# A selective-scan and attention block on one core: the front of the next image pair beside the phases behind a pair's scan

## The chip, the cores and the metric

The kernel runs on one core of a Trainium2 chip. The metric is the device time in microseconds (us) of one execution. The host only lays the inputs out, in one launch.

## The reference

Eight images of 96 channels and 64 x 64 points go through two layers. Shortened to what is computed:

```python
# layer 0: group norm, then a four-direction selective scan
xh = layernorm(gn(x) as tokens); xi, z = split(xh @ in_proj_w.T + in_proj_b)   # 192 + 192
xi = silu(depthwise_conv3x3(xi) + conv_b)
for k in range(4):                       # row order, column order, and both reversed
    dts, Bs, Cs = split(x_proj_w[k] @ xs[k])
    delta = softplus(dt_proj_w[k] @ dts + dt_proj_b[k])
    h_t = exp(delta_t * A) * h_(t-1) + delta_t * u_t * B_t        # 16 states a channel
    y_k = sum_n(h_t * C_t) + D * u
y = layernorm(sum of the four, back in row order) * silu(z)
x = x + (y @ out_proj_w.T + out_proj_b)
# layer 1 on the 4096 tokens of an image
t = x as tokens
t = t + attention(layernorm(t))          # linear: (q k^T / 4) v, no softmax, 6 heads
t = t + ffn(layernorm(t))                # 96 -> 384 -> 96, operands rounded to fp8 (5, 2)
```

Since the attention has no softmax, k^T v (16 x 16 for each head) is summed over all tokens first, and q times that sum is folded with the output weights into one 97 x 96 matrix for an image.

## The kernel before

The images go in four pairs. A pair's 4096 points are cut into 8 chunks of 512 (`F`, `NCH`). For each pair the function at the end of `vss_attn_ffn` calls, one after the other, `front`, `prepare`, `scan`, `back` and `tail`; each opens its own pools in SBUF and PSUM and closes them, and what passes between the stages lies in SBUF (`xi`, `t1`) or in scratch tensors in DRAM (`zs`, `us`, `dl`, `du`, `bs`, `cs`, `ys`).

- `front` loads an image (L240 statistics, L256 group norm), norms each chunk (L261 and L265 matmuls, L263 square, L267 Ln, L268 Exp, L269 and L270), projects it (L297, L299, L313 matmuls; L300 and L305 put the result into the padded images `ybuf`, L317 is the Silu of z, which goes to DRAM), and convolves: 9 taps on VectorE over whole images for two of the three tiles (`taps`, L281 and L283, then Silu, L286), and 9 diagonal matmuls a chunk for the third (L331, with Silu in the evacuation, L335). Its PSUM ring has four banks.
- `prepare` stores `xi` as `us` (L343 with `spread`), makes delta, its products and its three bf16 parts, and stores them.
- `scan` is under an order written out by hand. TensorE makes the decays (L553), ScalarE exponentiates them (L557), GpSimd makes the drive (L535), VectorE scans (L570), TensorE sums over the states (L588).
- `back` takes 16 steps, one for a chunk of an image. A step loads `z3`, `ut`, `xr` and `yk` (1.57 MB, four directions), adds directions (L686 on VectorE, L687 on GpSimd), transposes and sums them on TensorE into `py` (L691: two matmuls of 512 columns; L700: 64 small ones, four of which stand in different column groups), copies (L705, L707), norms (L713 `yc`, L716 square, L720 `yv`, L724, L725), gates (L729, L732), projects (L735 `po`) and adds the input (L738), into `t1` in SBUF. An fp32 matmul shows as two records in the profile. Each of `py`, `yc`, `yv`, `po` has two PSUM banks.
- `tail` first norms every chunk of `t1` into `tn` (L755 to L763) and sums k^T v (L780 `pk`, L785 `kv`, L789 `pm`); then forms the matrix `hm` for each image (L797 to L806); then runs the feed-forward over 16 steps, three at a time, as generators (L814 `pa`, L816, `norm`, L823 to L827, L831 to L838, store at L839).

Outside of `scan` a scheduler puts the instructions of each engine in order, from the order in the program and its own estimate of when operands are ready. All DMAs are issued by SP, in one order. Exp and Ln are in one table of ScalarE, Silu and Softplus in two others; a token (`stamp_issue_order_token`) keeps a table load in place.

Of the kernel before, what the change touches and what calls it, by code (L numbers as in the profile page):

```python
# [10 lines left out]
F32 = mybir.dt.float32  # L11
# [40 lines left out]
def vss_attn_ffn(ctx: ExitStack, tc: tile.TileContext, a: dict):  # L52
# [119 lines left out]
    def half(T):  # L172
        return 1 if T == 2 else 0

    def decay_weights():
# [42 lines left out]
    def front(pair, xi, zs, ybuf):  # L218
        with ExitStack() as st:
            p1 = st.enter_context(tc.tile_pool(name="p1", bufs=1))  # L220
            tmp = st.enter_context(tc.tile_pool(name="p1t", bufs=2))
            ps = st.enter_context(tc.tile_pool(name="p1ps", bufs=4, space=PSUM))

            diag = p1.tile([128, 9, 128], F32, name="diag")
            for t in range(9):
                nc.vector.tensor_scalar(
                    diag[:, t, :], ident, convw[:, 0, t : t + 1], None, ALU.mult
                )
            pad = [t.rearrange("p (h w) -> p h w", w=HH + 2) for t in ybuf]
            for t in ybuf:  # L230
                nc.gpsimd.memset(t, 0.0)

            xts = []
            for b in range(2):
                xt = p1.tile([DIM, L], F32, name="xt", bufs=2)
                xts.append(xt)
                nc.sync.dma_start(xt, x[2 * pair + b])
                bst = tmp.tile([DIM, NCH, 6], F32, name="bst")
                for c in range(NCH):
                    nc.vector.bn_stats(bst[:, c, :], xt[:, bass.ts(c, F)])  # L240
                mv = tmp.tile([DIM, 2], F32, name="mv")
                nc.vector.bn_aggr(mv, bst.rearrange("p c s -> p (c s)"))
                gps = ps.tile([128, F], F32, name="gps", tag="ps")
                nc.tensor.matmul(gps[:DIM, 0:1], gmat, mv[:, 0:1], start=True, stop=True)
                gm = tmp.tile([DIM, 1], F32, name="gm")
                nc.vector.tensor_copy(gm, gps[:DIM, 0:1])
                gd = tmp.tile([DIM, 1], F32, name="gd")
                nc.vector.tensor_tensor(gd, mv[:, 0:1], gm, ALU.subtract)
                gv = tmp.tile([DIM, 1], F32, name="gv")
                nc.vector.scalar_tensor_tensor(gv, gd, gd, mv[:, 1:2], ALU.mult, ALU.add)  # L250
                vps = ps.tile([128, F], F32, name="vps", tag="ps")
                nc.tensor.matmul(vps[:DIM, 0:1], gmat, gv, start=True, stop=True)
                gr = tmp.tile([DIM, 1], F32, name="gr")
                nc.scalar.activation(gr, vps[:DIM, 0:1], AF.Ln, bias=eps5[:DIM])
                nc.scalar.activation(gr, gr, AF.Exp, scale=-0.5)
                nc.vector.tensor_scalar(xt, xt, gm, gr, ALU.subtract, ALU.mult)  # L256

                for c in range(NCH):
                    cs = bass.ts(c, F)
                    cps = ps.tile([128, F], F32, name="cps", tag="ps")  # L260
                    nc.tensor.matmul(cps[:DIM], c96, xt[:, cs], start=True, stop=True)  # L261
                    sq = tmp.tile([DIM, F], F32, name="sq")
                    nc.scalar.activation(sq, cps[:DIM], AF.Square)  # L263
                    vp = ps.tile([128, F], F32, name="vp", tag="ps")
                    nc.tensor.matmul(vp[:DIM], j96, sq, start=True, stop=True)  # L265
                    rs = tmp.tile([DIM, F], F32, name="rs")
                    nc.scalar.activation(rs, vp[:DIM], AF.Ln, bias=eps5[:DIM])  # L267
                    nc.scalar.activation(rs, rs, AF.Exp, scale=-0.5)  # L268
                    nc.vector.tensor_tensor(xt[:, cs], cps[:DIM], rs, ALU.mult)  # L269
                    nc.vector.tensor_scalar(xt[:, cs], xt[:, cs], nw, nb, ALU.mult, ALU.add)  # L270


            def taps(T):

                for t in range(9):
                    dy, dx = divmod(t, 3)
                    w = convw[:, half(T), t : t + 1]
                    v = pad[T][:, dy : dy + HH, dx : dx + HH]
                    o = xi[T].rearrange("p (h w) -> p h w", w=HH)
                    if t == 0:  # L280
                        nc.vector.tensor_scalar(o, v, w, None, ALU.mult)  # L281
                    else:
                        nc.vector.scalar_tensor_tensor(o, v, w, o, ALU.mult, ALU.add)  # L283
                for c in range(NCH):
                    xc = xi[T][:, bass.ts(c, F)]
                    nc.scalar.activation(  # L286
                        xc, xc, AF.Silu, bias=convb[:, half(T) : half(T) + 1]
                    )

            for b in range(2):  # L290
                xt = xts[b]
                lo = slice(64 * b, 64 * b + 64)
                for c in range(NCH):
                    cs = bass.ts(c, F)
                    r0 = c * ROWS
                    pm = ps.tile([128, F], F32, name="pm", tag="ps")
                    nc.tensor.matmul(pm, winT[:, 0:128], xt[:, cs], start=True, stop=True)  # L297
                    pl = ps.tile([128, F], F32, name="pl", tag="ps")
                    nc.tensor.matmul(pl[lo], winT[:, 128:DI], xt[:, cs], start=True, stop=True)  # L299
                    nc.scalar.activation(  # L300
                        pad[b][:, r0 + 1 : r0 + 1 + ROWS, 1 : HH + 1],
                        pm.rearrange("p (h w) -> p h w", w=HH),
                        AF.Identity, bias=inb[:, 0:1],
                    )
                    nc.scalar.activation(  # L305
                        pad[2][lo, r0 + 1 : r0 + 1 + ROWS, 1 : HH + 1],
                        pl[lo].rearrange("p (h w) -> p h w", w=HH),
                        AF.Identity, bias=inb[lo, 1:2],
                    )
                    zt = tmp.tile([DIM, 2, F], F32, name="zt")  # L310
                    for g in range(2):
                        pz = ps.tile([128, F], F32, name="pz", tag="ps")
                        nc.tensor.matmul(  # L313
                            pz[:DIM], winT[:, DI + g * DIM : DI + (g + 1) * DIM], xt[:, cs],
                            start=True, stop=True,
                        )
                        nc.scalar.activation(  # L317
                            zt[:, g], pz[:DIM], AF.Silu, bias=inz[:, g]
                        )
                    nc.sync.dma_start(zs[b, :, :, cs].rearrange("g p l -> p g l"), zt)  # L320

                if b == 0:
                    taps(0)

            taps(2)
            for c in range(NCH):
                r0 = c * ROWS
                pc = ps.tile([128, F], F32, name="pc", tag="ps")
                for t in range(9):
                    dy, dx = divmod(t, 3)  # L330
                    nc.tensor.matmul(  # L331
                        pc, diag[:, t, :], pad[1][:, r0 + dy : r0 + dy + ROWS, dx : dx + HH],
                        start=(t == 0), stop=(t == 8),
                    )
                nc.scalar.activation(xi[1][:, bass.ts(c, F)], pc, AF.Silu, bias=convb[:, 0:1])  # L335
# [10 lines left out]
    def prepare(pair, xi, us, dl, du, bs, cs_):  # L346
        with ExitStack() as st:
# [8 lines left out]
            for o in range(2):  # L356
                for c in range(NCH):
# [12 lines left out]
                    for k in (o, o + 2):  # L370
# [12 lines left out]
                        for T in range(3):  # L383
# [5 lines left out]
                            act = nc.scalar.activation(  # L389
                                d, pq, AF.Softplus, bias=dtb[:, k, half(T) : half(T) + 1]  # L390
                            )
# [22 lines left out]
            tc.stamp_issue_order_token(act.ins, f"tables{pair}")  # L414


    def scan(pair, dl, du, bs, cs_, ys):
        with ExitStack() as st:
            st.enter_context(tc.manual_schedule())

            act = nc.scalar.preload_act_table_set(LOGEXP)
            tc.stamp_issue_order_token(act.ins, f"tables{pair}")
# [121 lines left out]
            def decay(p):  # L544
# [12 lines left out]
                act = nc.scalar.activation(e, e, AF.Exp)  # L557
                if p == 0:
                    tc.stamp_issue_order_token(act.ins, f"tables{pair}")
# [64 lines left out]
            for s in range(N + 2):  # L624
                for v in range(8):
# [22 lines left out]
                    next(more, None)  # L648


    def back(pair, ys, us, zs, t1):
        with ExitStack() as st:
            tmp = st.enter_context(tc.tile_pool(name="bk", bufs=2))
            psy = st.enter_context(tc.tile_pool(name="bky", bufs=2, space=PSUM))
# [88 lines left out]
    def tail(pair, t1):  # L743
        with ExitStack() as st:
# [5 lines left out]
            def bank(name):  # L750
                return ps.tile([128, F], F32, name=name, tag="ps")
# [233 lines left out]
```

## Time and profile before

| | us |
|---|---|
| median of 3 runs | 12261.4 (12260.9 to 12297.62) |
| profiled execution | 12263.4 |
| its span | 12261.5 |
| VectorE busy | 8797.7 |
| TensorE busy | 8871.2 |
| GpSimd busy | 7971.1 |
| ScalarE busy | 6823.8 |

The page lists for each line of the kernel the engine, the operation, the tiles, how often it ran, its busy time and mean duration, and the idle time before it with what ended it. A table by stretches shows the same busy times for any part of the span. The granted clock is the share of TensorE's full clock that the chip let through; matmul durations in the trace grow as it falls, and a mean over several stretches mixes both. A record of the trace is one instruction[...].

### The profile page before, as it was taken

The numbers are of one execution on the slowest core, as the hardware profiler recorded it, in microseconds if no ns is written. First come the engines' busy times: TensorE is split into PE (matmuls) and PEld (weight loads), VectorE is DVE, ScalarE is ACT, GpSimd is POOL, SyncE is SP. The second block draws the span as 40 slices with busy tenths as digits, with TensorE's granted clock in tenths as the row PEclk, the third lists the DMA queues.
The fourth block names the chain that finished last, engine by engine and source line by source line (L and its number), as shares of the span: only waits on it lengthen the run. The fifth ranks groups of instructions, "written<-read, shape, count | busy, mean of one in ns | idle before, by whom it ended". The sixth has DMA issues, their size and how long they took to land. (4 is left out here: it accounts for less than half of the span.)

```text
span 12261.5 us, 386934 instructions
## 1 busy us (share of the span) xinstructions
PE 8871.2 (72%) x170112; PEld 5730.0 (47%) x170112; DVE 8797.7 (72%) x6393; ACT 6823.8 (56%) x12095; POOL 7971.1 (65%) x2750
## 2 busy tenths in 40 slices
PE   6856666678886666667888666666778766666777
PEld 2245555543225555554322555555432255555543
DVE  4489999952448899995244899989424499999942
ACT  3566666633456666663345666666333566666623
POOL 0489999941048999993114899999300499999931
PEclk9678888887767878888775888888877688888887
DMA  2988888872298888887129888888712988888871
GB/s 74 203 199 199 199 198 198 198 164 49 63 211 200 199 194 197 203 198 154 41 73 203 198 200 198 198 196 201 157 36 67 217 198 200 198 199 203 199 157 24
DMA packets 1627242, 2042.53 MB, mean 167 GB/s; under 512 B 958083, under 2 KB 1303252, under 8 KB 1622740
## 3 DMA queue, kind: packets, MB, share of 16 engines
q1 hardware_dynamic: 1625556, 2017.78, 72.0%
q8 instruction: 1335, 21.87, 0.9%
q14 instruction: 351, 2.88, 0.1%
HBM read 1579.00 MB, written 438.38 MB: 165 GB/s over the span
## 5 line engine op out<-in xcount | busy, mean ns | idle before, releaser
L570 DVE TENSOR_TENSOR_SCAN h<-da,dbu 128x774 f32<-128x774 f32 x4096 | 7027.3, 1760 | 665.5 <-ACT da L557 522.2
L535 POOL TENSOR_TENSOR dbu<-dut,bc 128x1536 f32<-128x1536 f32 x2048 | 7084.7, 3504 | 594.0 <-ACT dbu L532 515.2
L557 ACT ACTIVATE da<-da 128x768 f32<-128x768 f32 x4096 | 3257.9, 798 | 2166.0 <-PE da L553 2123.5
L588 PE MATMUL yp<-h,cw 128*32 128x48 f32 x131072 | 3142.9, 246 | 1130.8 <-issue 1115.7
L553 PE MATMUL da<-dm,aw 128*128 128x128 bf16 x24576 | 2508.0, 251 | 1458.0 <-DVE h L570 1076.1
L588 PEld LDWEIGHTS yp<-h,cw 128*32 128x32 f32 x131072 | 2545.6, 155 | 1699.1 <-issue 1431.7
L553 PEld LDWEIGHTS <-aw 128*128 128x128 bf16 x24576 | 1846.8, 111 | 1768.5 <-issue 1439.4
L489 ACT ACTIVATE cw<-bc,blk 128x512 f32<-128x512 f32 x2048 | 1475.1, 722 | 309.8 <-DMA bc<-cs 230.5
L408 POOL TENSOR_TENSOR dp<-rest,dp 128x512 bf16<-128x512 f32 x384 | 458.4, 1194 | 718.7 <-ACT dp L407 688.0
L406 DVE TENSOR_TENSOR rest<-delta,dp 128x512 f32<-128x512 f32 x384 | 302.5, 789 | 674.5 <-ACT dp L405 674.5
L687 POOL TENSOR_TENSOR yk<-yk 128x768 f32<-128x768 f32 x64 | 143.5, 2243 | 942.4 <-DMA yk<-ys 480.4
L365 POOL COPY u<-xi 128x512 f32<-128x512 f32 x96 | 111.0, 1170 | 982.7 <-PE pc L331 653.4
L385 PE MATMUL pq<-S,dtw 12*128 12x512 f32 x768 | 594.8, 882 | 167.0 <-ACT S L377 91.6
L838 POOL TENSOR_TENSOR ot<-t,y 96x512 f32<-96x512 f32 x64 | 73.5, 1148 | 944.1 <-DVE y L836 929.1
L596 ACT ACTIVATE yev<-yp 128x384 f32<-128x384 f32 x1024 | 503.6, 492 | 242.6 <-PE yp L588 240.9
L385 PEld LDWEIGHTS pq<-S,dtw 12*128 12x128 f32 x768 | 162.5, 251 | 596.6 <-ACT delta L389 182.8
L407 ACT ACTIVATE dp<-rest 128x512 bf16<-128x512 f32 x384 | 241.4, 630 | 323.6 <-DVE rest L406 323.6
L532 ACT COPY dbu<-h 128x12 f32<-128x12 f32 x1984 | 408.3, 206 | 0.0
L729 DVE SCALAR_TENSOR_TENSOR g<-yc,c_onw,yrs 96x512 f32<-96x512 f32 x128 | 89.8, 741 | 443.3 <-ACT yrs L725 443.3
L707 ACT ACTIVATE yt<-py 128x512 f32<-128x512 f32 x64 | 38.2, 597 | 662.9 <-PE py L700 590.1
L700 PE MATMUL py<-ident,yk 128*24 128x128 f32 x8192 | 291.1, 310 | 26.4 <-DVE yk L686 26.2
L700 PEld LDWEIGHTS py<-ident,yk 128*24 128x24 f32 x8192 | 256.8, 118 | 113.5 <-DVE yk L686 78.2
(131 smaller groups left out, 6892.3 us busy)
## 6 DMA issues: line engine op xcount, KB each, us to landing
dut<-du SPq DMA_DIRECT2D x1024, 768.0 KB
dm<-dl SPq DMA_DIRECT2D x512, 576.0 KB
dl<-dp SPq DMA_DIRECT2D x256, 384.0 KB
dm<-dl SPq DMA_DIRECT2D x512, 192.0 KB
ys<-yev SPq DMA_DIRECT2D x1024, 96.0 KB
du<-du SPq DMA_DIRECT2D x256, 256.0 KB
bc<-bs SPq DMA_DIRECT2D x512, 128.0 KB
bc<-cs SPq DMA_DIRECT2D x512, 128.0 KB
```

Of the source, the lines that this page charges most:

```text
L385: nc.tensor.matmul(pq, dtw[64:76, k, T], S[64:76], start=True, stop=True)
L406: nc.vector.tensor_tensor(rest, d, dp[:, :, 0], ALU.subtract)
L408: nc.gpsimd.tensor_tensor(dp[:, :, 2], rest, dp[:, :, 1], ALU.subtract)
L489: nc.scalar.activation(cw[i % 2][:, :, :, m, :].rearrange("p z j t -> p (z j) t"), bc[i][:, 1].rearrange("p z (j t) -> p (z j) t", j=NB), ...
L532: nc.scalar.copy(start, segs(hs[s - 1][:, :, r])[:, :, :, 1 if back else TC])
L535: nc.gpsimd.tensor_tensor(segs(t)[:, :, :, 1:], dut[g // 2][:, NI * (r % 2) : NI * (r % 2) + NI, :].unsqueeze(1) .to_broadcast([128, 2, NI ...
L553: nc.tensor.matmul(e[:, i], aw[k, r][:, i, z, :], dm[s][:, NI * r + i, :], start=True, stop=True,)
L557: act = nc.scalar.activation(e, e, AF.Exp)
L570: nc.vector.tensor_tensor_scan(hs[s][:, w, r][:, d], da[p % 3][:, o : o + W6][:, d], dbu[4 * s + r][:, w][:, d], 0.0, ALU.mult, ALU.add,)
L588: nc.tensor.matmul(y[32 * q : 32 * q + 32, 2 * NE * i : 2 * NE * i + 2 * NE] .rearrange("p (j r i) -> p i j r", j=2, r=NR), w[:, z, :, t], ...
L596: nc.scalar.activation(yev[s][:, :, o : o + 8, :].rearrange("p j i e -> p i j e"), y[:, 0 : 16 * NE].rearrange("p (i j e) -> p i j e", j=2 ...
L700: nc.tensor.matmul(o, yk[:, k, 4 * g + e, NE * j : NE * j + NE], ident, start=False, stop=(k + j == 4),)
```

## The change

The loop over pairs now runs `npair + 1` times. In round n the phases behind the scan of pair n - 1 and the front of pair n run together, in two parts, and then `prepare` and `scan` of pair n follow as before. `front` is cut into generators: `project` (load, norm, projection; 34 pieces) and `convolve` (19 pieces), and the Silu of the convolution becomes a function of its own, `gates`. `back` and `tail` are generators too, and `together` takes pieces of one and of the other in turn:

```diff
+    def together(one, other, n, m):
+        done = 0
+        for i in range(n):
+            next(one, None)
+            while done * n < (i + 1) * m:
+                next(other, None)
+                done += 1
...
+                one = other = none
+                if old:
+                    one = back(
+                        pair - 1, old["ys"], old["us"], old["zs"], old["t1"], old["tn"],
+                        pool("bk", 2), pool("bky", 1, space=PSUM), pool("bkc", 2, space=PSUM),
+                        pool("bkm", 1, space=PSUM), pool("bkp", 2, space=PSUM),
+                    )
+                if new:
+                    other = project(
+                        pair, new["zs"], ybuf, pool("p1", 1, side="right"),
+                        pool("p1t", 2, side="right"), pool("p1ps", 2 if old else 6, space=PSUM),
+                    )
+                together(one, other, 16 if old else 1, 34)
...
+                if old:
+                    one = tail(
+                        pair - 1, old["t1"], old["tn"], pool("tt", 3), pool("tps", 6, space=PSUM)
+                    )
+                if new:
+                    other = convolve(
+                        xi, ybuf, pool("p1c", 1, side="right"), pool("p1cp", 2, space=PSUM)
+                    )
+                together(one, other, 18 if old else 1, 19)
...
+                gates(xi)
+                prepare(xi, new["us"], new["dl"], new["du"], new["bs"], new["cs"])
```

PSUM is divided anew: `py` has one bank, `yc` two, the attention sums of both images one, and `yv`, `po` and all of the attention part share a ring of two; `project` has two more beside `back` and six in the first round. The attention sums follow each chunk of `back` one step later, and `t1` and `tn` pass through DRAM:

```diff
+            def heads(i, b, ta):
+                c = i // 2
+                to = tns[i % 3]
+                norm(ta, to[0:DIM], tmp, bank)
+                nc.sync.dma_start(tn[b, :, bass.ts(c, F)], to[0:DIM])
+                for n in range(2):
+                    pk = bank("pk")
...
+                    ta = tmp.tile([DIM, F], F32, name="ta")
+                    nc.vector.scalar_tensor_tensor(ta, po[:DIM], outb, xr, ALU.add, ALU.add)
+                    nc.sync.dma_start(t1[b, :, cs], ta)
+                    if late:
+                        heads(*late)
+                    late = (2 * c + b, b, ta)
+                    yield
...
             def ffn(b, c):
                 cs = bass.ts(c, F)
+                to = tns[(2 * c + b) % 4]
+                nc.sync.dma_start(to[0:DIM], tn[b, :, cs])
+                ta = tmp.tile([DIM, F], F32, name="ta")
+                nc.sync.dma_start(ta, t1[b, :, cs])
                 pa = bank("pa")
-                nc.tensor.matmul(pa[:DIM], hm[b], tn[b][:, cs], start=True, stop=True)
+                nc.tensor.matmul(pa[:DIM], hm[b], to, start=True, stop=True)
```

The taps run over half images, a chunk of the diagonal matmuls stands behind every second tap and is evacuated without Silu, and `gates` applies it afterwards. Table loads are placed by one helper for the whole program, which keeps Ln/Exp, Silu and Softplus in the order in which the program names them:

```diff
+    def table(kind, emit):
+        if kind == "ln" and loaded[0] != "ln":
+            act = nc.scalar.preload_act_table_set(LOGEXP)
+            tc.stamp_issue_order_token(act.ins, "tables")
+        loaded[0] = kind
+        act = emit()
+        if act is not None:
+            tc.stamp_issue_order_token(act.ins, "tables")
...
+        for T in (0, 2):
+            for t in range(9):
+                dy, dx = divmod(t, 3)
+                w = convw[:, half(T), t : t + 1]
+                for h in (0, HH // 2):
...
+                if t % 2:
+                    chunk()
+                yield
+
+    def gates(xi):
+        for c in range(NCH):
+            for T in range(3):
+                xc = xi[T][:, bass.ts(c, F)]
+                b_ = 0.0 if T == 1 else convb[:, half(T) : half(T) + 1]
+                table("silu", lambda: nc.scalar.activation(xc, xc, AF.Silu, bias=b_))
```

`prepare` and `scan` change only in how they name their table loads. What each piece computes is the same as before.

## The prediction

> **What bounds the kernel now.** I read the page first, then the table by stretches for the border between the first and the second pair, then one step of the second half in order of time. The page:
>
> ```profile
> PE 8871.2 (72%) x170112; PEld 5730.0 (47%) x170112; DVE 8797.7 (72%) x6393; ACT 6823.8 (56%) x12095; POOL 7971.1 (65%) x2750
> ...
> DVE  4489999952448899995244899989424499999942
> ...
> PEclk9678888887767878888775888888877688888887
> ...
> L570 DVE TENSOR_TENSOR_SCAN h<-da,dbu 128x774 f32<-128x774 f32 x4096 | 7027.3, 1760 | 665.5 <-ACT da L557 522.2
> ```
>
> Four times the digits of DVE fall from 9 to 2 or 4 and come back: four scans of about 1900 us each, bound by DVE (and POOL), with some 1110 us of other stages between two of them. The change leaves the scan alone, so only those stages count. The stretches from one scan's end to the next one's begin (columns: stretch, length, busy us of PE, PEld, DVE, ACT, POOL with instruction counts, granted clock, DMA share, GB/s):
>
> ```profile
> 2582.00:2861.00 279.00, 225.87 (x2370) 114.39 (x2370) 89.58 (x112) 49.85 (x81) 34.17 (x16) 0.90 0.76 149
> 2861.00:2947.00 86.00, 71.91 (x324) 44.76 (x324) 12.49 (x23) 43.44 (x80) 6.95 (x2) 0.94 0.00 1
> 2947.00:3125.00 178.00, 133.23 (x194) 36.98 (x194) 60.47 (x147) 64.89 (x112) 18.26 (x16) 0.52 0.06 17
> 3125.00:3150.00 25.00, 0.94 (x5) 0.82 (x5) 20.74 (x23) 0.46 (x2) 11.17 (x4) 0.50 0.56 134
> 3150.00:3222.00 72.00, 57.94 (x66) 15.54 (x66) 24.78 (x41) 28.43 (x47) 0.00 (x0) 0.50 0.00 0
> 3222.00:3289.00 67.00, 66.32 (x132) 19.92 (x131) 28.08 (x11) 46.82 (x68) 0.00 (x0) 0.92 0.30 88
> 3289.00:3352.00 63.00, 62.22 (x146) 27.22 (x145) 50.30 (x12) 16.04 (x26) 0.76 (x1) 1.00 0.18 56
> 3352.00:3690.00 338.00, 275.16 (x384) 71.60 (x383) 149.88 (x198) 189.90 (x322) 147.56 (x122) 0.66 0.96 215
> ```
>
> In order: back, attention sums, feed-forward, load of x, layer norm, in-projection, convolution, prepare. The first seven take 770 us and PE is the busiest engine in six of them; but it runs at half clock in two (0.52, 0.50), where it waits in chains through ACT and DVE. So overlap can win twice: waits are filled, and the clock may rise. Prepare runs at DMA share 0.96 and stays as it is. One step of back:
>
> ```profile
> 2702.93 3.69 PE L700 MATMUL py<-ident,yk 128*24 128x128 f32 x128
> ...
> 2706.57 3.67 PE L713 MATMUL yc<-yt,c 128*96 128x512 f32 x8
> ...
> 2710.08 1.94 PE L720 MATMUL yv<-sq,j 96*96 96x512 f32 x4
> ...
> 2711.86 1.88 PE L691 MATMUL py<-ut,dpad 96*128 96x512 f32 x4
> ...
> 2715.55 1.96 PE L735 MATMUL po<-g,c_woT 96*96 96x512 f32 x4 [1.81 <-DVE g L732]
> ...
> 2717.44 3.69 PE L700 MATMUL py<-ident,yk 128*24 128x128 f32 x128
> ```
>
> An undisturbed step is 14.51 us (2702.93 to 2717.44), nearly all PE: 20 records of 512 columns and 128 small ones. The 16 steps take 255 us, 16 each: lower clock and late yk account for the rest.
>
> [...] The trace shows 1283 ns for each of its loads[...].
>
> **The change, part by part.** PE prices at full clock: a 512-column fp32 record is 0.43 us (convolution: 144 records in 62 us), a small py record 0.027 (3.42 us of weight loads for 128), pk 0.16 and pm 0.08 by their columns.
>
> Phase one puts `project` (load, norm, in-projection of the next pair) beside `back`, and the attention sums of a chunk (`heads`) one step behind it. It replaces 279 + 86 + 25 + 72 + 67 = 529 us. PE work per step: back 20 x 0.43 + 3.4 = 12.0; heads 4 x 0.43 + 8 x 0.16 + 8 x 0.08 = 3.6; project has 192 records, 82 us, or 5.1 a step: 20.7 in all, 331 us for 16 steps. That is the floor. The waits come from smaller rings: py has one bank instead of two, yv, po, ncp, nvp, pk share two, project has two.
>
> The order holds two kinds of steps. One with two norm chunks, in us after the end of yv: cps to 0.85; py to 1.7; vp waits for its Square, which stands on ACT behind Ln and Exp (0.68, 0.63): 2.35 to 3.2; 12 small py to 3.85; po to 5.55; ncp to 6.4; nvp after its Square, 7.4 to 8.25; the second half of py waits for the DVE copy out of the only bank: 9.7 to 10.55; the second cps waits until DVE has freed its bank, behind two Ln/Exp pairs: 12.2 to 13.05; pk to 14.35; pm and vp to 16.1; py to 16.95; yc waits for ACT's copy, behind another Ln/Exp: 18.05 to 21.5; yv to 23.4. The other kind has two in-projection chunks: pm, pl, py, two pz fill the wait for g to 4.3; po and ncp to 6.85; nvp from 7.85; pk waits for Ln, Exp and the multiply, 11.3 to 12.6; pm, pl, pz, pz with their evacuations to 16.9; py to 18.6; yc waits for two Silu, a table load and the copy, 19.9 to 23.3; yv to 25.2. Mean 24.3. The clock of back is 0.90[...]; at 0.95 the 20.7 us of work grow by 1.1: I take 25.5 a step. Phase one = 19 us to the first py (2582 to 2601) + 16 x 25.5 + 10 for the last heads = 437.
>
> What hides there: 16 table loads per pair (20 us of ACT; the walk has both of a step on the chain for about 1 us[...]). DMA moves at most 3.7 MB a step (2.55 for back, 0.4 for t1 and tn, 0.8 for zs), 147 GB/s in 25 us where prepare shows 215. On SP, a step's last yk loads are queued behind the stores of t1, tn and zs, which wait for DVE and ACT; issued about 14 us into a step they are wanted 11 us later, so they land just in time. If they were 3 us late, 48 us a pair.
>
> Phase two puts the convolution beside feed-forward: 178 + 63 = 241 us before. DVE becomes the bound: 36 half taps of 2.25 us (L283, 4.48 for a whole one) less two short ones, 77, and 16 x 4.1 for feed-forward (t2, tq, three each of h16 and hq, y16), 142. In the order some 3.2 half taps stand in a step until they run out after about 11 steps. Walk of such a step: t2, hq, two half taps to 5.9; tq waits for Exp until 7.0; y16, half tap to 10.3; the three h16/hq to 12.25. So 11 x 12.3 + 5 x 10 (10.9 now at half clock) + 10 for the hm chain and the reload from DRAM = 195. PE has 9.5 us of work in such a step at full clock; at half clock it would be 19 and dense[...].
>
> Then 24 Silu of 0.7 us, taken out of the convolution's evacuation and L286, stand alone on ACT before prepare's own work: 15 us with the table load. All of us is stored at that point; before, xi0 (2.1 MB, 10 us at 215 GB/s) had gone out earlier, and prepare is DMA-bound: I add 8. Lead 23, between 15 and 35.
>
> Sum per border: 437 + 195 + 23 = 655 against 770, 115 less, three times 345. The last pair has no partner: back with heads walks to 20 us a step, I take 21: 19 + 336 + 10 = 365, the same as 279 + 86; 5 more for the DRAM reload in feed-forward. First pair: same work, the conv still follows the projections: 0, plus or minus 15. From the profiled execution's 12263.4 (span 12261.5, 2 above the median of the runs): 12263 - 345 + 5 = 11923, and with the 2 us to the median, 11920.
>
> **Rivals.** (a) Waits fill better than the walk says: 21.5 us a step, close to the PE floor, and phase two 170: 19 + 344 + 10 + 170 + 20 = 563, 207 saved three times: 11645. For it: the PE floor[...]. (b) The queues cost more[...]: 28 us a step and 215 in phase two: 477 + 215 + 23 = 715, 55 saved three times: 12100. For it: POOL's 480 us of waits for yk already now; against: DMA share well below 1. (c) Slower: in phase one the granted clock falls to half as in the feed-forward. Then a step has 41 us of PE work, 44 with the waits, phase one 733, and the time is 12800 if it lasts; the change loses from 32.7 us a step on (552 us for phase one), that is, when about half of the steps run at half clock. For it: 0.50 in both norm stages; against: back holds 0.90 with the same dense py, yc, yv. (d) The order doesn't overlap as it says: excluded as far as the order goes, since project stands between the py of back on every engine; little but a wash is left, 12260.
>
> **How the numbers follow.** Forecast 0.64, (a) 0.12, (b) 0.15, (c) 0.07, (d) 0.02. The forecast's own spread (step 24 to 27, phase two 180 to 215, lead 15 to 35) is 11800 to 12040. The range 11690 to 12130 reaches into (a) and over (b). Faster, by over 0.3% (37 us, about what a measurement of this kernel can tell): 0.91; within 0.02; slower 0.07.
>
> **What would show it.** Right: steps of py 24 to 27 us apart with yc waiting for the copy; clock 0.9 or more; feed-forward steps of 12 us with DVE at over 0.9, later 10 or less; prepare still 338 with some 20 us before its first activation. Wrong: steps under 22 or above 30, clock 0.5 in phase one, POOL waiting for yk in most steps, or a scan of another length.

## The result and the profile after

| us | before | after |
|---|---|---|
| median (4 runs each) | 12261.85 (12260.9 to 12297.62) | 11829.53 (11820.4 to 11864.4) |
| profiled execution | 12263.4 | 11820.4 |
| start to first scan | 668.5 | 638.8 |
| four scans | 7649.2 | 7629.6 |
| from a scan's end to the next scan, three times | 1124.9, 1141.4, 1138.9 | 993.0, 994.2, 988.4 |
| last scan's end to the end | 538.6 | 574.4 |

A scan is counted from VectorE's first scan instruction to the start of ScalarE's last copy of its sums.

The ratio is 0.9646 (95% interval 0.962 to 0.9672). The profiled executions differ by 443.0 us: 29.7 at the start, 19.6 in the scans (a scan takes 1900 to 1926 us in all runs of this document, so this is scatter), 429.6 in the three borders, and 35.8 lost behind the last scan. The page after:

```profile
PE 8675.0 (73%) x170112; PEld 5662.7 (48%) x170112; DVE 8756.4 (74%) x6465; ACT 6900.1 (58%) x12176; POOL 7986.7 (68%) x2770
...
DVE  5489999963549999995355999999454699999922
...
PEclk8678888879768888888976888888896788888896
...
L588 DVE TENSOR_TENSOR_SCAN h<-da,dbu 128x774 f32<-128x774 f32 x4096 | 7028.4, 1760 | 646.5 <-ACT da L577 443.1
```

The scan's row has hardly moved (7027.3 us before, 7028.4 now). The low stretches of DVE between the scans are shorter and no longer fall to 2. The first border by stretches (columns as before; the scan ends at 2540.6):

```profile
2541.00:2983.00 442.00, 401.60 (x2921) 186.86 (x2921) 134.92 (x205) 187.68 (x294) 44.58 (x26) 0.93 0.58 131
2983.00:3055.00 72.00, 68.20 (x172) 27.59 (x171) 72.00 (x76) 26.61 (x46) 16.97 (x6) 1.00 0.20 58
3055.00:3110.00 55.00, 38.88 (x78) 13.23 (x79) 45.36 (x52) 20.32 (x36) 13.35 (x5) 0.73 0.17 50
3110.00:3168.00 58.00, 42.07 (x64) 11.58 (x62) 20.77 (x51) 25.32 (x44) 6.09 (x6) 0.56 0.10 31
3168.00:3188.00 20.00, 17.39 (x29) 6.10 (x30) 4.86 (x6) 18.74 (x33) 7.78 (x8) 0.76 0.47 194
3188.00:3533.00 345.00, 269.19 (x374) 71.26 (x373) 145.57 (x193) 189.39 (x320) 147.68 (x120) 0.63 0.98 216
```

Phase one (first row) has TensorE called busy 402 of 442 us at clock 0.93. Phase two (rows two to four) has DVE busy 72 of 72 us in its first stretch, where the taps are thickest; when they and the convolution's matmuls are gone, the clock falls to 0.56 and the feed-forward goes on alone, 10.9 us a step as before. Row five is the lead, row six the prepare, as before at a high DMA share (0.98; it was 0.96). One in-projection step of phase one in order of time (start, duration, engine; from one `ta` to the next):

```profile
2713.62 0.75 DVE L796 SCALAR_TENSOR_TENSOR ta<-po,c_outb,xr 96x512 f32<-96x512 f32 x1 [2.25 <-PE po L792]
...
2717.64 1.28 ACT L305 ACT_TABLE_LOAD   x1
...
2719.80 1.02 PE L285 MATMUL pm<-xt,c_winT 96*128 96x512 f32 x2
...
2722.43 1.96 PE L301 MATMUL pz<-xt,c_winT 96*96 96x512 f32 x4
...
2727.06 3.67 PE L771 MATMUL yc<-yt,c 128*96 128x512 f32 x8
...
2735.27 1.88 PE L301 MATMUL pz<-xt,c_winT 96*96 96x512 f32 x4
...
2736.99 1.88 PE L792 MATMUL po<-g,c_woT 96*96 96x512 f32 x4
...
2738.90 0.75 DVE L796 SCALAR_TENSOR_TENSOR ta<-po,c_outb,xr 96x512 f32<-96x512 f32 x1 [2.24 <-PE po L792]
```

A step is 25.28 us. The project's matmuls stand between those of `back`: `pz` fills the time in which `g` is made, and `po` follows directly. TensorE is busy nearly all of this step (the same columns):

```profile
2713.62:2738.90 25.28, 24.56 (x185) 11.48 (x184) 5.72 (x8) 13.51 (x20) 1.83 (x1) 1.00 0.62 147
```

### The profile page after: what moved, and what is told of

It is laid out like the page before. It is cut to its first block, busy times and chain, and to the rows that moved or that the text cites. A ratio compares the mean times of both kernels' runs of the same rounds, so it can differ in the third digit from the quotient of the medians.

```text
span 11818.4 us, 387513 instructions
## 1 busy us (share of the span) xinstructions
PE 8675.0 (73%) x170112; PEld 5662.7 (48%) x170112; DVE 8756.4 (74%) x6465; ACT 6900.1 (58%) x12176; POOL 7986.7 (68%) x2770
## 5 line engine op out<-in xcount | busy, mean ns | idle before, releaser
L588 DVE TENSOR_TENSOR_SCAN h<-da,dbu 128x774 f32<-128x774 f32 x4096 | 7028.4, 1760 | 646.5 <-ACT da L577 443.1
L745 POOL TENSOR_TENSOR yk<-yk 128x768 f32<-128x768 f32 x64 | 115.8, 1809 | 1268.2 <-DMA yk<-ys 1010.6
L858 POOL TENSOR_TENSOR ot<-t,y 96x512 f32<-96x512 f32 x64 | 128.1, 2002 | 612.0 <-DVE y L856 593.7
L672 ACT ACTIVATE nsq<-ncp 96x512 f32<-96x512 f32 x128 | 75.8, 592 | 572.8 <-PE ncp L670 559.6
L758 PEld LDWEIGHTS py<-ident,yk 128*24 128x24 f32 x8192 | 231.6, 108 | 241.7 <-issue 182.6
L758 PE MATMUL py<-ident,yk 128*24 128x128 f32 x8192 | 319.1, 290 | 31.5 <-DVE yk L744 25.7
```

The costliest lines, as they stand in the source:

```text
L588: nc.vector.tensor_tensor_scan(hs[s][:, w, r][:, d], da[p % 3][:, o : o + W6][:, d], dbu[4 * s + r][:, w][:, d], 0.0, ALU.mult, ALU.add,)
L758: nc.tensor.matmul(o, yk[:, k, 4 * g + e, NE * j : NE * j + NE], ident, start=False, stop=(k + j == 4),)
```

## The experiments

Each edit is against the changed kernel. A border is the time from one scan's end to the next scan (mean of three in the changed kernel: 991.9 us). Phase one runs from the scan's end to the first `pa` (442.4, 442.0 and 433.7 us, mean 439.4), phase two from there to the first `pt` of prepare (mean 185.5). The traces give these to a few us; the whole time of a single run also holds the scatter of the scans. The four first runs shared a chip on which the kernel before took 12308.71 in one run; it took 12307.79 (median of 7) beside the next four, 12251.66 (of 9) beside the next three, and 12274.91 beside the last.

**How much each overlap is worth: one phase at a time made serial.** In the first, `back` runs to its end before `project` starts (with six PSUM banks); in the second, `tail` before `convolve`.

```diff
-                    one = back(
+                    for _ in back(
...
+                    ):
+                        pass
+            with ExitStack() as st:
...
-                    other = project(
+                    for _ in project(
```

> Phase one without the overlap: back with the attention sums is closed before the pools of project open (six banks for it, as in the first round); phase two is untouched. If the overlap of phase one carries the gain, each of the three borders gets longer by about 391 (back with heads alone, as in the last pair) + 177 (project alone, as in the first pair) - 442 (phase one now) = 126 us, up to 150 with the load of x, and the kernel comes to 12200 to 12280 us, no better than before the change. Rival, that phase two and the shorter first pair carry it: under 60 us a border, below 12010 us.

> Phase two without the overlap: the convolution's tiles take the place of the feed-forward's, so it starts when that has ended; phase one is untouched. If VectorE was filled by the overlap, phase two goes from 185 us to 178 for the feed-forward and 63 to 80 for the convolution, 241 to 260 us: 55 to 75 us more for each of three borders, 11995 to 12055 us. Rival, that the overlap only trades waits (the merged steps were as long as the plain ones): under 20 us a border.

Measured: 12069.81 and 12056.4; borders 1074.6, 1076.8, 1078.5 (mean 84.7 more) and 1062.0, 1065.6, 1068.7 (73.5 more). A border gained 143.2 us by the change; without the first overlap 58.5 of that is left, without the second 69.7. The second came out as expected, phase two 243 us in the mean and the rest in the lead. The first came out below what was expected: phase one was 114 us longer, but phase two became 32 shorter (152 to 154), though none of its code had changed. In that run 26 of the 36 half taps had already run before phase two began, the first of them 451 us after the scan's end, while `project` stood alone. The long taps (L344) before and behind the first `pa` (stretch, length, DVE's busy time in them with their number, granted clock, DMA share, GB/s):

```profile
2986.00:3090.00 104.00, 50.65 (x22) 0.75 0.20 58
3090.00:3243.00 153.00, 23.77 (x11) 0.88 0.20 58
```

One tap lies across the cut, and four short ones (L342) ran before it. So this run is not phase one made serial and nothing else: part of the convolution had moved beside `project`, and 84.7 us is too low a price for the first overlap (114 in phase one itself). In the changed kernel 3 half taps run before the first addition `t2` (L836) of the feed-forward, and 3 or 4 stand in each of its first ten steps. The stretches of phase two in the serial run (columns as in the border's table):

```profile
3090.00:3190.00 100.00, 99.04 (x260) 41.05 (x261) 63.15 (x104) 47.13 (x83) 15.60 (x10) 1.00 0.24 70
3190.00:3243.00 53.00, 35.97 (x65) 10.39 (x64) 20.82 (x52) 26.26 (x45) 6.00 (x6) 0.66 0.12 34
```

DVE is busy 63 of 100 us here, TensorE all the time at full clock. The first steps, with taps, took 10.6 to 10.9 us, the next ones, with the convolution's matmuls and no tap, 8.1 to 8.3. So the taps are what lengthens a step while those matmuls run. Whether they cost as much when they are evenly spread this run can't say; the next one does. Its expectation, written before this was seen, takes the short phase two for a sign of better order.

**The taps spread on purpose.** A token binds the order of the half taps and of the addition `t2`, two half taps to a step:

```diff
+                    tc.stamp_issue_order_token(tap.ins, "taps")
...
-                nc.vector.tensor_tensor(t2, ta, pa[:DIM], ALU.add)
+                add = nc.vector.tensor_tensor(t2, ta, pa[:DIM], ALU.add)
+                tc.stamp_issue_order_token(add.ins, "taps")
```

> The half taps of the convolution are bound in order to ffn's additions on VectorE, two to a step. Theory A (phase two is long because VectorE does its taps bunched in the first steps, leaves the rest of ffn to a stretch at a low TensorE clock, and a spread keeps both busy; in the run with phase one serial the same phase took 152 us at a full clock): phase two of a border 185 us falls to 150 to 165, the whole 11720 to 11770. Rival B (a tap then stands in the chain of each step; 18 steps of 11 us or more): phase two 190 to 200, the whole 11835 to 11870. If the clock falls to half in spite of the spread: 185, no change.

Measured: 11781.24; borders 963.6, 965.1, 965.1 (27.3 less), phase two 160, 159 and 159. Phase two of its first border in two stretches, and then the same cut in the changed kernel:

```profile
2998.40:3098.00 99.60, 96.58 (x252) 39.68 (x251) 82.75 (x117) 47.59 (x83) 11.50 (x10) 0.99 0.24 70
3098.00:3158.60 60.60, 42.50 (x63) 11.76 (x62) 47.98 (x61) 23.34 (x39) 7.73 (x5) 0.50 0.10 29
```

```profile
2983.00:3101.00 118.00, 100.65 (x240) 38.75 (x239) 115.20 (x123) 43.92 (x76) 29.53 (x10) 0.91 0.19 54
3101.00:3168.00 67.00, 48.49 (x73) 13.65 (x73) 22.93 (x57) 28.32 (x48) 6.88 (x6) 0.55 0.12 35
```

With the spread, DVE has slack in the first stretch (83 of 100) and the steps take 9.1 us at clock 0.99; about a third of the taps moves into the second stretch, where DVE was busy only 23 of 67 us. Those steps keep their 10.9 us at half clock with two taps in most of them: the taps cost nothing there. So how the taps were bunched had set the length of phase two. The clock falls 6 us after the last convolution matmul, which ends 525 us after the scan's end; in the changed kernel it falls 5 to 7 us after them, in the run with phase one serial 10 to 16.

The serial run shows one more place for taps: VectorE is busy 135 of 442 us in phase one, and the taps of the first image need only that image's projections. No run tried them there beside `back`, where `xi` has no buffers yet.

**Is phase one bound by ScalarE, the loads of data, or TensorE?** Three runs. The first writes z through Exp instead of Silu, which removes 16 table loads a border; the second issues `back`'s first step before `project` begins; the third computes one half of z only and writes it twice.

```diff
-                    table("silu", lambda: nc.scalar.activation(
-                        zt[:, g], pz[:DIM], AF.Silu, bias=inz[:, g]
+                    table("ln", lambda: nc.scalar.activation(
+                        zt[:, g], pz[:DIM], AF.Exp, bias=inz[:, g]
```

> z is written through Exp in place of Silu, so the gate multiplies by exp(z) and not by silu(z): the Silu is left out, and with it 16 loads of activation tables in each of three borders (1.28 us each by the trace). Theory A (phase one is a chain through ScalarE, and half of its steps pay a load in the chain): phase one of a border 442 us falls by 8 x 1.28 = 10 to 16 x 1.28 = 20 us, to 422 to 432; the whole 11765 to 11800. Rival B (the loads lie in ScalarE's idle time): phase one stays at 435 to 442, the whole 11815 to 11840. [...]

```diff
+                if old:
+                    next(one, None)
-                together(one, other, 16 if old else 1, 34)
+                together(one, other, 15 if old else 1, 34)
```

> The first step of back is issued alone, ahead of project, so that project's first load of x (and its cast) stands behind that step's loads of y, u and z in the queues. Theory A (the 36 us second step of phase one is the wait for a load that x delayed): that step falls to 26 us, phase one from 442 to 430 to 434, the whole about 11800. Rival B (x then comes later for project, and project's last step ends as much later): phase one stays within 3 us, the whole 11820 to 11840.

```diff
-                    pz = ps.tile([128, F], F32, name="pz", tag="fps")
-                    nc.tensor.matmul(
+                    if g == 0:
+                        pz = ps.tile([128, F], F32, name="pz", tag="fps")
+                        nc.tensor.matmul(
```

> z is computed for one of its two halves and that half is written twice: one matmul of 96x512 a chunk, 16 a border (some 0.95 us each by the timeline), is left out; ScalarE, VectorE and the DMAs keep all their work. Theory A (in phase one TensorE's queue is full and sets the step): phase one 442 us falls by 12 to 18 us, the in-projection steps from 25.3 to 23.5-24.4. Theory B (the step is a chain through the other engines or SyncE's queue, and z's matmuls stand beside it): phase one within 4 us, as it was without the table loads.

Measured: 11868.36, 11872.98 and 11834.28, times that tell little beside the scans' scatter; phase one tells more. Without the table loads it is 436.3, 434.4, 439.7 (mean 436.8, 2.6 less), and the in-projection steps keep 25.3 us, though ScalarE's busy time in the stretch fell from 188 to 167. So rival B of that run holds, and the loads, 1283 ns each, do not stand in the chain. With x behind the first step, 440.7, 440.4, 439.8: the second step of the first border did fall from 36.3 to 19.3 us, but the third rose from 24.2 to 33.9, and the later steps gave the rest back. With half of z's matmuls gone, 426.5, 422.8, 430.2 (mean 426.5, 12.9 less), and seven in-projection steps of the first border together 163.2 us instead of 177.1 (a step between them got 5 us longer). That is 2.0 us a step, and what was taken from TensorE is 1.96 a step (half of `pz`, 1.96 a chunk, two chunks). So TensorE's queue is the path through these steps, as its 24.56 busy us of 25.28 had it, and ScalarE's table loads lie in ScalarE's idle time.

**The ring through SyncE.** In the trace, the loads of `yk` for two steps on stand in SyncE's queue behind the store of `ta` and the load of `xr`, which waits for it. The run moves the load of `xr` behind those of `yk` (with the larger last ring and the spread taps in):

```diff
-                    xr = tmp.tile([DIM, F], F32, name="xr")
-                    nc.sync.dma_start(xr, x[2 * pair + b, :, cs])
...
+                    xr = tmp.tile([DIM, F], F32, name="xr")
+                    nc.sync.dma_start(xr, x[2 * pair + b, :, cs])
                     nc.vector.tensor_tensor(yk[:, 0], yk[:, 0], yk[:, 2], ALU.add)
```

> The last pair's larger ring and the spread taps of the two earlier runs, and besides: in back, xr is loaded after yk, so that in SyncE's queue the loads of yk two steps on no longer stand behind a load that waits for ta. Theory A (the steps of back are a ring of two steps through ta, the loads of yk behind it in SyncE's queue, and the sums on yk): a step of the last pair falls from 20.5 to 18 us or less, the last pair from 552-559 to 520 or less; in phase one, too, the steps fall. Theory B (a step is TensorE's own queue, in order, with what it waits for inside a step): last pair 545 to 560, phase one within 8 us of 435-442.

Measured: 11740.44; the last pair 543.6 us to its last `ot` against 548.8 in the run with the other two edits alone. A steady step stays at 20.5 us in both; of the 5 us 1.7 come from the first step and 2.8 from two late ones. Phase one 437.3, 434.2, 434.2. So the place of xr's load is not what bounds a step. The store of `ta` still stands ahead of the loads of `yk` in SyncE's queue in this run, so the edit alone does not rule the ring out. The trace tells more. A steady step of the last pair, TensorE's stretch from one `po` to the next, and the one long wait in it:

```profile
11362.10:11382.60 20.50, 17.69 (x169) 9.25 (x169) 5.72 (x9) 5.99 (x10) 1.81 (x1) 1.00 0.68 145
...
11382.60 1.96 PE L793 MATMUL po<-g,c_woT 96*96 96x512 f32 x4 [1.82 <-DVE g L790]
```

Besides the 17.69 us of work TensorE waits 1.82 for `g`, 0.68 for ScalarE's Square and 0.30 for `tn`, and in this step not at all for `yk`. So it is TensorE's queue, with what it waits for inside the step (theory B), that sets a step here.

**The last pair's PSUM.** In the last round nothing shares PSUM, so `py` gets two banks and the common ring three:

```diff
-                        pool("bk", 2), pool("bky", 1, space=PSUM), pool("bkc", 2, space=PSUM),
-                        pool("bkm", 1, space=PSUM), pool("bkp", 2, space=PSUM),
+                        pool("bk", 2), pool("bky", 1 if new else 2, space=PSUM), pool("bkc", 2, space=PSUM),
+                        pool("bkm", 1, space=PSUM), pool("bkp", 2 if new else 3, space=PSUM),
```

> Only in the last round, where no front runs beside: two banks for py instead of one and three in the shared ring instead of two. If the last pair got 36 us longer because the one bank makes the second half of py wait for the copy, and the ring the attention part, its steps fall from 20.9 to 17.5 to 19 us and the last pair gets 30 to 50 us shorter; the rest stays, 11780 to 11800 us. Rival, that the step is bound by TensorE's own work (15.6 us) and the chain through ACT and DVE whatever the banks: steps stay above 20 us, no change.

Measured: 11830.34; last `ot` at 555.0 instead of 570.2, 15 less, half of what was expected. A steady step went from 20.9 to 20.5 us only; most of the gain is in the first steps. With these banks what holds a step at 20.5 us is what the trace above shows, TensorE's work and its waits for `g`; no run took one of these away.

**The first pair: place of the call, or side of the buffers?** In the kernel before, the prepare of the first pair waited 52.2 us for the stores of the decay weights, `awd`; in the changed one it does not. First the call is put back behind the convolution:

```diff
                 together(one, other, 16 if old else 1, 34)
-            if pair == 0:
-                decay_weights()
...
                 together(one, other, 18 if old else 1, 19)
+            if pair == 0:
+                decay_weights()
```

> The decay weights are made after the convolution of the first round, right before prepare, as they were before the change, instead of between project and convolve. If that move gave the shorter first pair (its scan starts 30 us earlier), the first scan starts 45 to 65 us later than in the changed kernel, since its front is itself some 28 us slower than before; 11875 to 11895 us. Rival, that the cut of the front into generators gave it: first scan within 10 us of the changed kernel's.

Measured: 11836.16, first scan at 651.5 us (638.8 in the changed kernel; 626 to 639 in the other runs whose first round is the same, 622 and 648 in the two that change z). That is some 13 us more, not much beyond that scatter, and not 45 or more; nobody waits for `awd`. So the expectation was wrong about the cause. The second run keeps this and lets the first round's `project` and `convolve` take their SBUF on the left again, where `decay_weights` takes its own:

```diff
-                        pair, new["zs"], ybuf, pool("p1", 1, side="right"),
+                        pair, new["zs"], ybuf, pool("p1", 1, side="right" if old else "left"),
...
-                        xi, ybuf, pool("p1c", 1, side="right"), pool("p1cp", 2, space=PSUM)
+                        xi, ybuf, pool("p1c", 1, side="right" if old else "left"), pool("p1cp", 2, space=PSUM)
```

> As the run with the decay weights behind the convolution, but the first round's front (project's and convolve's SBUF pools) stands on the left side again, where the decay weights' buffers then take its place. Theory A (in the kernel before, the decay weights waited for the front's SBUF, and the prepare for theirs; the pools' new side, not the place of the call, took that wait away): the four stores of awd start behind the front, at 280 to 320 us of the span (at 97 to 195 with the pools on the right), the prepare's first S waits 40 to 55 us for them, and the first scan starts at 675 to 700 us (651.5 with the pools on the right, 668.5 in the kernel before). Rival B (the stores went early because the queue was free): stores of awd before 200 us, first scan at 635 to 655 us.

Measured: 11912.39, first scan at 695.9, all as theory A has it. The stores of `awd` in this run, and who waited for them:

```profile
L235 SPq DMA_DIRECT2D awd<-awp x4: 320/323/329, 304.9 to 332.5; - x4
...
  ACT S L396: 46.8, 1
```

and the same in the run with the right side (nobody waits there):

```profile
L235 SPq DMA_DIRECT2D awd<-awp x4: 349/390/413, 96.2 to 195.2; - x4
```

On one side, buffers freed by one stage are taken by the next, so the decay weights had to wait for the front to leave, and the prepare for them. On two sides neither waits. This is a part of the change that its description doesn't name. With both edits the first scan starts 27 us later than in the kernel before (668.5), though the order of buffers is the old one again: the first round's front, as rewritten, is itself slower there, where nothing runs beside it.

**Together.** All three edits, spread, last ring and x behind the first step, timed in three rounds; then spread and last ring alone, in five.

> The last pair's larger ring of PSUM buffers, x's load behind the first step of back, and the spread taps together: the sum of what each gave, 15 us at the end, 0 to 30 from x, -30 to 100 from the taps. Theory A (both theories A of the two single runs): 11690 to 11760. If only the ring helps: 11800 to 11820. If the taps stand in the chain: 11850 or more.

> The last pair's larger ring and the spread taps alone, without the changed load of x: border 960 to 966 us (993 in the changed kernel, 964 with the taps alone) and the last pair 552 to 560, so 11765 less what the scans vary by: 11740 to 11790. If the gain of the single look at the taps was the scans' scatter, 11810 or more.

Measured: 11788.01 (11772.06 to 11812.02), ratio to the kernel before 0.9581 (0.955 to 0.9611); and 11719.81 (11715.31 to 11750.86), ratio 0.9563 (0.9532 to 0.9594). The second has borders of 968.9, 970.6 and 960.8 and its last `ot` 548.8 us after the last scan. Both intervals lie below that of the changed kernel (0.962 to 0.9672), each taken beside its own runs of the kernel before: these two edits beat both kernels. The intervals of the two versions overlap, and their borders (970.7 and 966.8 in the mean) differ by less than a prepare does between runs (314 to 337 us from GpSimd's first `dp` to its last): the moved load of x is not shown to matter.

## Why the prediction was right, and where it was off

The mechanism was right: both phases got shorter because waits were filled, and in phase two the clock rose with it (0.52 in the feed-forward and 1.00 in the convolution before, 0.65 over their 241 us by length; 0.78 over the 185 us that the two take together now in the first border). That it would rise was the author's estimate. The time fell inside the forecast's own spread, 90 us below its middle. Its sum was -345 for the borders, +5 for the last pair, 0 for the first; measured, with the scans' -19.6 apart, -429.6, +35.8 and -29.7. In part these errors cancel, which was luck: without the 31 us that the last pair lost beyond the forecast, the median would have been 11799, at the edge of that spread.

- **Phase one, 437 us:** measured 439.4. Its two kinds of steps, 23.4 and 25.2 in the walk, are 22.0 to 24.3 and 24.4 to 26.0, apart from the second step (27 to 36 us, for the load of `yk`). The walk assumed that each engine works in the order of its queue. The clock is 0.93, so the slower rival (c), half clock, is out, and no step but the second reached (b)'s 28 us. The table loads, of which the walk put 1 us a step on the chain, cost about nothing: the run without them gained 2.6 us in all. In the trace 49 of the 62 loads of tables behind the program's first begin 0.02 us after an activation and end 0.01 to 0.02 us before the next. One sign that was named for a wrong forecast, GpSimd waiting for `yk`, did appear (1010.6 us of its idle time over the 64 steps), but it was a poor sign: GpSimd had nothing else to do, and earlier loads did not shorten a steady step.
- **Phase two, 195 us:** 185.5. The steps with taps took 10.9 to 13.3 instead of 12.3, the later ones 10.9 instead of 10. "DVE becomes the bound" held for the order as it stood, 115 of 118 us; but it was no property of the work, as the spread showed: same operations, 159 to 160 us. (a)'s 170 for this phase was thus within reach, by another order than the one the change has.
- **Lead, 23 us:** the forecast adds it to a prepare of unchanged length, so what counts is the rise. From the first `pt` to GpSimd's first `dp` it is 19.1 us where the kernel before had 8.5, a rise of 10.6. This was the term that was off most, by 12. The Silus do take 16 us (3163.6 to 3179.9 in the first border), as the walk has it, but the first of them run before `pt`, beside the last steps of the feed-forward, and `pt` runs beside the rest. The prepare kept its length within scatter.
- **The border's baseline, 770 us:** it was read from one border; the mean of three is 775. Together: from the scan's end to GpSimd's first `dp` the three borders of before have 778.4, 779.6 and 793.8, mean 784, and now 644.0 in the mean, so 140 a border and not 115. Of the 25 more, 12 are the lead, 9.5 phase two and 5 the baseline, less 2.4 for phase one. The rest of the 429.6, 10 us, is in the prepares' own lengths.
- **Last pair, +5:** +35.8, of which phase two has 6, as forecast. The other 30 are in `back` with `heads`, where "16 x 21 + 10" was mis-sized. The steps were nearly right (21.5 in the mean, `back` done after 364 us), but the last heads and the matrix `hm` behind them took 27 us and not 10. Without a partner, heads inside the steps hide nothing: the steps grew from 15.8 to 21.5 us in the mean, 85 us together, about all of the 87 that the sums and `hm` had taken behind them, and yet 27 us stayed behind.
- **First pair, 0 within 15:** -29.7. The trace of before had the 52.2 us wait for `awd`, but the forecast took the work as unchanged and did not ask which buffers the decay weights wait for. The side of the pools removed it.

## What to carry to other kernels

- When two stages are to run side by side, look at which engine each stretch leaves idle, then spread the small operations of the partner evenly over all of it: bunched taps kept VectorE busy 115 of 118 us and then 23 of 67, and one token that spread them brought 27 us a border.
- Read a baseline from every repetition, and count a delay as the rise over what the same stretch took before: a lead of 23 us was a rise of 10.6, an error larger than that of either phase's walk.
- A run that takes one overlap away is no clean price before its trace shows that nothing moved into the gap: here 26 half taps had.
- Where buffers lie can order stages that share no data: ask of each pool whose space it takes, and when that is left.

## What the runs showed of the hardware

GpSimd's addition `ot` takes 1.15 us, but 3.14 to 3.27 where a tap of VectorE starts 0.15 to 0.21 us before it: so it is for 27 of the 48 in the three borders of the changed kernel, and each of the other 21 takes 1.15. Two neighbouring operations in the changed kernel, and one of the last steps, without a tap:

```profile
3014.65 2.34 DVE L344 SCALAR_TENSOR_TENSOR xi<-y,c_convw,xi 128x2048 f32<-128x2048 f32 x1
3014.81 3.19 POOL L858 TENSOR_TENSOR ot<-t,y 96x512 f32<-96x512 f32 x1 [10.01 <-DVE y L856]
...
3109.21 1.15 POOL L858 TENSOR_TENSOR ot<-t,y 96x512 f32<-96x512 f32 x1 [9.28 <-DVE y L856]
```

The tap ends at 3016.99, and `ot` at 3018.00, 1.01 us later, close to the 1.15 that `ot` takes without a tap. In the run with phase two serial, the 16 of a border take 1148 ns each in the mean; in the first border of the changed kernel 2288; with the taps spread, ten take 11.50 us together in the first of the two stretches shown above, and five 7.73 in the second. No other engine's work waits for `ot` here, so it cost nothing.

The granted clock, stage by stage: 0.99 and 1.00 where the convolution's matmuls fill the feed-forward's gaps (TensorE busy 96.58 of 99.60 us with the taps spread, 68.20 of 72 in the changed kernel), 0.50 and 0.56 in the stretches after they end (called busy 42.50 of 60.60 and 42.07 of 58), and 0.52 with the feed-forward alone in the kernel before (133.23 of 178). What sets it, no run showed.

In the kernel before, an fp32 record of TensorE with 96 x 512 operands takes 594 ns (`yv` at 2710.1 to 2711.4, clock 1.00) and 1061 and 1166 ns (`cps` and `vp` at 3160 to 3175, clock 0.50), each in the median. A record of the dense convolution lasts 592 ns, while 144 of them take 62.2 us, 0.43 us for each. The 128 matmuls into `yv` show as 256 records.

Each table load takes 1283 ns, in the kernel before and in the changed one. The kernel before has 14: the first activation table, one for the Exp of the decay weights, and four each in front of the Silu of z, of the Softplus, and behind the Softplus for the return to Ln and Exp; none stands between a Ln and its Exp, which begins within 0.03 us of it in the mean (L761 and L762).
